# A fused cross-attention block in float32: its steps in a new order, and idle transposes in ten groups instead of two

## The chip, the cores and the metric

The kernel runs on one core of one Trainium2 chip. The metric is the device time of one execution in microseconds (us), as the median of several runs. Before the change it is 1016.84 us, the median of three runs between 1015.93 and 1018.15.

The core has five engines with instruction queues of their own: TensorE (PE in the profile; its weight loads stand apart as PEld), VectorE (DVE), ScalarE (ACT), GpSimd (POOL) and SyncE (SP), which here only issues DMAs. Each queue is worked off in the order of the program, and engines wait for one another by semaphores.

## The reference, cut to what matters

Queries come from `x` (16 batches of 1024 rows, 512 wide), keys and values from a context of 64 rows for each batch. Both are normalised and then scaled and shifted by a condition vector.

```python
def _ada_ln(x, c, W_ss, b_ss):
    mu = jnp.mean(x, axis=-1, keepdims=True)
    var = jnp.mean((x - mu) ** 2, axis=-1, keepdims=True)
    h = (x - mu) / jnp.sqrt(var + EPS)
    ss = jax.nn.silu(c) @ W_ss + b_ss
    scale, bias = jnp.split(ss, 2, axis=-1)
    return (1.0 + scale)[:, None, :] * h + bias[:, None, :]
...
xq = _ada_ln(x_q, t_vec, Wss_q, bss_q)
xkv = _ada_ln(x_kv, t_vec, Wss_kv, bss_kv)
q = (xq @ Wq + bq).reshape(B, Lq, nh, dh)
kv = (xkv @ Wkv + bkv).reshape(B, Lkv, 2, nh, dh)
...
scores = jnp.einsum('bqhd,bkhd->bhqk', q, k) / jnp.sqrt(jnp.float32(dh))
attn = jax.nn.softmax(scores, axis=-1)
out = jnp.einsum('bhqk,bkhd->bqhd', attn, v).reshape(B, Lq, H)
return x_q + (out @ Wp + bp)
```

There are 16 heads of width 32, and everything is float32.

## The kernel before

**Tiles.** The queries are cut into 32 blocks of 512 rows (`NB = 32`), two for each batch. The context is cut into two groups of eight batches, A and B, each as wide as one block. Features lie on the 128 partitions in four chunks (`NC = 4`).

**Seven products.** Each of the projections (keys, values, queries, output) is computed as seven half-size products in place of eight, from sums and differences of half matrices. `seven` (L551) does it for keys, values and queries, `product` (L911) for the output. Products 1, 6, 5 and 3 add up in one PSUM bank, 2 in one of its own, 7 and 4 in another, and what a bank holds is taken out between two products that add into it: `query_out` (ACT, L590) after 2, 6, 7 and 3, `query_added` (DVE, L597) after 5 and 4. So product 4 can start only when `query_out(n, 7)` has read the bank. Sums of features are made by `feature_sums` in four steps (L507; step 2 gives the operand of product 6, step 3 that of product 4), those of weights by `column_sums` (GpSimd, L481), those of attention rows by `row_sums` (GpSimd, L879 to L891).

**Way in.** `load_first` and `load_scale_shift` fetch the first context rows and the weights of scale and shift; `condition_turned` and `silu` prepare the condition; `q_stats`, `first_scale` and `hidden` normalise; `turned_features` transposes on TensorE; `scale_shift_rows`, `scale_shift_taken` and `scale_shift` make scale and shift; `modulated` applies them. Then come the 14 products of the context group A (`context_product`), mixed with those of query block 0, and those of group B, mixed with blocks 1 and 2. `biases(k)` transposes a few rows of biases into PSUM bank 1 on TensorE and copies them out on DVE (L236 to L243); the products k2 and k7 of group A use bank 1 too. `warm_up(n)` makes n transposes of the identity into a bank that nothing reads (L969).

**Loop.** `for i in range(3, NB - 2)` runs 27 times. In iteration i there are the scores of block i in two halves (`score_products`, L669), each with its column maxima (`maximum` on DVE, L686), a copy from PSUM to SBUF (`copied` on ACT, L695), an exchange of rows (`exchanged` on ACT, L724), `maxima` (DVE, L706 and L715), `subtract` (GpSimd, L732), `weights` (exponentials on ACT, L736) and `row_total` (DVE, L745); the mix with the values of block a = i - 1 (`mix`, L813), divided by its row sums (`inverse`, `spread_rows`, `divided` on DVE) and its output products 1, 2, 6, 5, 7; the output products 3 and 4 of block b = i - 2; the seven query products of block n = i + 1; and for later blocks the normalisation (`q_stats`, `q_scale`, `hidden`), a transposition by DVE and 16 DMAs (`turn`, `move`), scale and shift (`scale_features`, L456) and feature sums. `take` (ACT, L952) and `joined` (GpSimd, L957) bring an output product into the residual rows, as `added` (DVE, L931 and L936) does for others. The scores use both pairs of PSUM banks of the pool `ps_s`, and so does the mix: each waits until the copies and maxima, or `divided`, have emptied them.

**Way out.** Blocks y = 30 and z = 31 are written out by hand after the loop.

**What sets the order.** The order is written out: under `manual_schedule` each engine gets its instructions in the order in which the program's steps issue them. A step is a call such as `query_product(n, 4)`, and the change consists of such calls in another order.

Of the kernel before, what the change touches and what calls it, by code (L numbers as in the profile page):

```python
# [11 lines left out]
ALU = mybir.AluOpType  # L12
# [8 lines left out]
def cross_attention_block(  # L21
# [943 lines left out]
    warm = bank("warm", 1)  # L965

    def warm_up(n):
        for _ in range(n):
            nc.tensor.transpose(warm[:, :P], ident, ident)  # L969
# [39 lines left out]
    modulated("A", 1, 0, nc.vector)  # L1009
    turned_features("A", 2)  # L1010
    load_context_weights(1, 0, 1)
    modulated("A", 0, 1, nc.scalar)
    load_context_weights(0, 1)
    load_biases(1)
    load_scale_shift("q", w_ss_q, 0)
    load_scale_shift("q", w_ss_q, 1)
    q_stats(0, (3,))
    modulated("A", 1, 1, nc.vector)
    q_stats(0, (1,))
    q_stats(0, (2,))  # L1020
# [36 lines left out]
    hidden(0, (1,))
    hidden(0, (2,))
    context_out("A", "k", 6)
    q_stats("B", (2,))  # L1060
    q_stats("B", (1,))
    hidden(0, (0,))
    context_product("A", "k", 5)
    column_sums("q", w_q_sb, w_q_sums, (0,))
    turned_products()
    turned_scaled(0)
    context_out("A", "k", 5)
    context_out("A", "v", 1)
    load_x(1)
    context_product("A", "k", 3)  # L1070
    turned_scaled(1)
    q_stats("B", (3,))
    context_product("A", "v", 6)
    q_stats("B", (0,))
    context_out("A", "v", 2)
    turned_scaled(3)
    q_scale("B")
    context_out("A", "k", 4)
    context_out("A", "k", 3)
    context_product("A", "v", 7)  # L1080
    context_out("A", "v", 6)
    turned_scaled(2)
    hidden("B", (1,))
    hidden("B", (3,))
    query_product(0, 1)
    hidden("B", (0,))
    turned_features("B", 1)
    turned_features("B", 3)
    query_seed(0)
# [3 lines left out]
    turned_features("B", 0)  # L1093
    column_sums("q", w_q_sb, w_q_sums, (2,))
    hidden("B", (2,))
    query_product(0, 2)
    q_stats(1, (0,))
    q_stats(1, (2,))
    q_stats(1, (1,))
    q_stats(1, (3,))  # L1100
    q_scale(1)
    feature_sums(0, nc.gpsimd, (2,))
    column_sums("q", w_q_sb, w_q_sums, (1,))
    turned_features("B", 2)
    load_x(2)
    query_out(0, 2)
    modulated("B", 0, 0, nc.vector)
    modulated("B", 0, 1, nc.vector)
    context_out("A", "v", 7)
    hidden(1, (0,))  # L1110
    context_product("A", "v", 5)
    hidden(1, (3,))
    query_product(0, 7)
    context_product("A", "v", 4)
    modulated("B", 1, 1, nc.vector)
    hidden(1, (2,))
# [316 lines left out]
    for i in range(3, NB - 2):  # L1433
# [10 lines left out]
        if next_x:  # L1444
            q_stats(i + 4, (1,))
# [284 lines left out]
```

## Time and profile before

| what | value |
|---|---|
| median of three runs | 1016.84 us |
| the profiled execution | 1016.95 us |
| its span in the profile | 1015.1 us |
| busy: TensorE, DVE, GpSimd, ACT | 988.8, 920.1, 811.9, 771.1 us |
| way in, up to the first scores of block 3 | 160.3 us |
| loop, 27 iterations | 782.1 us |
| way out | 72.7 us |

The profiled execution took 1.85 us more than its span, which runs from the first instruction to the last. Times in the views are microseconds from the span's start. Busy time of TensorE is modelled: matmuls are pipelined and their shown lengths overlap, so a product's cost is read from start to start. A group's idle time is the wait of its engine just before it, with what ended that wait.

### The profile page before, as it was taken

To read this page: it belongs to the slowest core of one execution; us is meant where nothing else is said; L and a number is where in the kernel's file an instruction comes from. 1 tells how busy PE (TensorE), PEld (TensorE's weight loads), DVE (VectorE), ACT (ScalarE), POOL (GpSimd) and SP (SyncE) were. 2 spreads that over 40 slices of the span, in tenths; PEclk is the share of its full clock that TensorE was granted. 3 is DMA by queue.
4 is the path that set the end of the run, shared out by engine and by line. 5 is a ranking of instruction groups with operands and counts; after the bars stand their busy time and mean duration, and the time that the engine had idled before them with its cause. 6 is when DMAs were issued, how large, how long until landed. Compare 5 with 4: busy or idle time off the path is not lost. (4 is left out here: it accounts for less than half of the span.)

```text
span 1015.1 us, 17766 instructions
## 1 busy us (share of the span) xinstructions
PE 988.8 (97%) x6060; PEld 760.6 (75%) x6060; DVE 920.1 (91%) x1170; ACT 771.1 (76%) x1426; POOL 811.9 (80%) x603
## 2 busy tenths in 40 slices
PE   6999999999999999999999999999999999999998
PEld 5788777777777777777777777777777777777666
DVE  6589999999999999999999999999999999987895
ACT  3588775778888877788888777887887778886651
POOL 2476685988888889888888898888888988888794
PEclk9999999999999999999999999999999999999999
DMA  9465634455555445555545455555454455445223
GB/s 318 151 190 146 174 117 140 128 159 154 169 152 146 134 133 156 161 155 167 158 140 139 127 158 160 154 164 166 133 137 134 151 163 157 120 127 159 80 71 128
DMA packets 111802, 151.71 MB, mean 149 GB/s; under 512 B 29624, under 2 KB 45008, under 8 KB 111712
## 3 DMA queue, kind: packets, MB, share of 16 engines
q1 hardware_dynamic: 111024, 149.75, 49.6%
q8 instruction: 49, 0.80, 0.3%
q0 software_dynamic: 256, 0.52, 0.2%
q14 instruction: 41, 0.34, 0.1%
q10 hardware_dynamic: 432, 0.30, 0.1%
HBM read 80.26 MB, written 35.65 MB: 114 GB/s over the span
## 5 line engine op out<-in xcount | busy, mean ns | idle before, releaser
L732 POOL TENSOR_TENSOR s<-s,mb 128x2048 f32<-128x2048 f32 x64 | 290.9, 4545 | 31.7 <-DVE mb L715 29.2
L911 PE MATMUL pp<-w_p_sb,ot 128*128 128x256 f32 x760 | 178.9, 379 | 0.0
L957 POOL TENSOR_TENSOR r<-r,taken 128x512 f32<-128x512 f32 x116 | 146.8, 1277 | 23.5 <-ACT taken L952 23.3
L911 PEld LDWEIGHTS pp<-w_p_sb,ot 128*128 128x128 f32 x760 | 144.4, 190 | 19.7
L590 ACT ACTIVATE qt<-pq,bias_t 128x256 f32<-128x256 f32 x256 | 104.3, 474 | 70.6 <-PE pq L551 69.9
L686 DVE TRANSPOSE_TENSOR_REDUCE m<-ps 128x32 f32<-128x1024 f32 x128 | 155.5, 1219 | 2.1 <-ACT s L695 1.0
L715 DVE STREAM_TRANSPOSE mb<-m 128x2048 f32<-128x2048 f32 x64 | 147.9, 2312 | 7.0 <-POOL s L879 0.5
L745 DVE TRANSPOSE_TENSOR_REDUCE lt<-s 128x64 f32<-128x2048 f32 x64 | 143.8, 2278 | 5.1 <-ACT s L736 5.1
L695 ACT COPY s<-ps 128x1024 f32<-128x1024 f32 x128 | 126.9, 1015 | 23.6 <-POOL r L957 12.7
L736 ACT ACTIVATE s<-s 128x2048 f32<-128x2048 f32 x64 | 122.6, 1915 | 3.6 <-POOL s L732 3.5
L551 PE MATMUL pq<-xt,w_q_sb 128*128 128x256 f32 x512 | 124.1, 385 | 0.4 <-ACT pq L563 0.4
L911 PE MATMUL pp<-WT,ot 128*128 128x256 f32 x512 | 123.9, 385 | 0.0
L551 PEld LDWEIGHTS pq<-xt,w_q_sb 128*128 128x128 f32 x512 | 94.7, 190 | 36.5 <-issue 21.1
L911 PE MATMUL pp<-WT,s 128*128 128x256 f32 x512 | 121.2, 380 | 0.4 <-DVE r L936 0.4
L551 PE MATMUL pq<-xt,w_q_sums 128*128 128x256 f32 x512 | 121.2, 379 | 0.0
L911 PEld LDWEIGHTS pp<-WT,ot 128*128 128x128 f32 x512 | 94.9, 190 | 34.6 <-issue 21.9
L551 PE MATMUL pq<-xt_sums,w_q_sums 128*128 128x256 f32 x512 | 116.5, 379 | 0.5 <-ACT qt L590 0.5
L911 PEld LDWEIGHTS pp<-WT,s 128*128 128x128 f32 x512 | 97.0, 190 | 16.0 <-POOL r L957 1.3
L551 PEld LDWEIGHTS pq<-xt,w_q_sums 128*128 128x128 f32 x512 | 97.1, 190 | 14.8 <-ACT qt L590 0.8
L551 PEld LDWEIGHTS pq<-xt_sums,w_q_sums 128*128 128x128 f32 x512 | 97.2, 190 | 14.1 <-ACT qt L590 0.9
L347 ACT ACTIVATE x<-x,rstdq 128x512 f32<-128x512 f32 x128 | 103.9, 819 | 1.8 <-POOL rstdq L322 1.1
L952 ACT COPY taken<-pp 128x512 f32<-128x512 f32 x116 | 68.0, 586 | 47.3 <-PE pp L911 47.2
(172 smaller groups left out, 1611.4 us busy)
## 6 DMA issues: line engine op xcount, KB each, us to landing
x<-in_x_dram SPq DMA_DIRECT2D x32, 1024.0 KB, 5.1
r<-in_x_dram SPq DMA_DIRECT2D x32, 1024.0 KB, 6.8
out_dram<-r SPq DMA_DIRECT2D x62, 512.0 KB, 7.7
xt<-ht SPq DMA_DIRECT2D x488, 64.0 KB, 2.0
wss_kv<-in_L_xcond_Wss_kv_dram SPq DMA_DIRECT2D x4, 512.0 KB, 7.5
wss_q<-in_L_xcond_Wss_q_dram SPq DMA_DIRECT2D x4, 512.0 KB, 8.0
ltd<-lt SPq DMA_DIRECT2D x32, 64.0 KB, 1.5
vr<-ltd SPq DMA_DIRECT2D x126, 16.0 KB, 1.7
```

Of the source, the lines that this page charges most:

```text
L347: nc.scalar.activation(dst, src, AF.Identity, bias=rstd[:, 1, j : j + 1], scale=rstd[:, 0, j : j + 1])
L551: nc.tensor.matmul(out_, lhsT=lhsT, rhs=rhs, start=new and m == 0 and c == 0, stop=c == HC - 1, skip_group_check=True,)
L590: nc.scalar.activation(dst, src, AF.Identity, bias=bq_t[:, o : o + 1])
L686: nc.vector.tensor_reduce(m_tiles[i][:, z, 0, 2 * e : 2 * e + 2, :], s_banks[i, z][e].rearrange("p r (j a) -> p r j a", a=32), AX.X, ALU.m ...
L695: nc.scalar.copy(s_tiles[i, z][:, 2 * e : 2 * e + 2, :], s_banks[i, z][e])
L715: nc.vector.transpose(t, src.unsqueeze(2).to_broadcast([P, HPC * NJ, 32]))
L732: eng.tensor_tensor(s_tiles[i, w], s_tiles[i, w], mb_tiles[i, w], ALU.subtract)
L736: nc.scalar.activation(p, p, AF.Exp, scale=SCALE)
L745: nc.vector.tensor_reduce(lt_tiles[i][:, :, w, :], s_tiles[i, w].rearrange("p r (j a) -> p r j a", a=32), AX.X, ALU.add, apply_transpose=True,
L911: nc.tensor.matmul(acc[products_of(i, n)][:, t * HO : (t + 1) * HO], lhsT=rows[:, c, t * P : (t + 1) * P], rhs=cols[:, c, :], start=new an ...
L952: nc.scalar.copy(taken[i][:, slot, :], acc[products_of(i, n)])
L957: nc.gpsimd.tensor_add(r, r, taken[i][:, slot, :].rearrange("p (t h) -> p t h", t=2))
```

## The change

`warm_up` gets a bank as its second argument and takes a fresh tile on every call. It is called for 12, 4, 4, 3, 3, 4, 4, 4, 4 and 4 transposes between the first steps, where it was called for 12 and 6. All other steps of the way in, the loop and the way out are kept and stand in a new order; in the way in that covers loads too (the weights of scale and shift ahead of the key weights, the projection's weights earlier), and `context_product("A", "k", 1)` and `2` come before the first of the values. The diff, cut to the first steps, the loop and a part of the way out:

```diff
@@ -962,730 +962,740 @@
 
     w_k_sums = big.tile([P, 4, HC, HO], F32, tag="big2", name="w_k_sums")
     w_q_sums = qpool.tile([P, 4, HC, HO], F32, tag="wq", name="w_q_sums")
-    warm = bank("warm", 1)
-
-    def warm_up(n):
+    warmed = []
+
+    def warm_up(n, k=1):
+        warmed.append(n)
+        warm = bank(f"warm_{len(warmed)}", k)
         for _ in range(n):
             nc.tensor.transpose(warm[:, :P], ident, ident)
 
 
 
-    condition_turned()
-    load_first(2, 2)
+    warm_up(12)
     q_stats("A", (0,))
     q_stats("A", (1,))
-    warm_up(12)
-    warm_up(6)
+    warm_up(4, 2)
+    load_first(2, 2)
+    load_scale_shift("kv", w_ss_kv, 0, (1,))
     first_scale(0)
+    warm_up(4, 2)
+    warm_up(3)
+    condition_turned()
+    silu()
+    q_stats("A", (3,))
+    q_stats("A", (2,))
+    load_biases(0)
+    load_scale_shift("kv", w_ss_kv, 1, (0,))
+    warm_up(3)
+    warm_up(4, 2)
+    biases(0)
+    warm_up(4, 2)
     load_scale_shift("kv", w_ss_kv, 0, (0,))
-    load_context_weights(0, 0, 0)
-    q_stats("A", (2,))
-    hidden("A", (1,))
-    q_stats("A", (3,))
-    silu()
+    load_scale_shift("kv", w_ss_kv, 1, (1,))
     first_scale(1)
     hidden("A", (0,))
-    turned_features("A", 0)
+    load_biases(1)
+    warm_up(4, 2)
     hidden("A", (2,))
-    load_scale_shift("kv", w_ss_kv, 0, (1,))
+    warm_up(4, 2)
+    warm_up(4, 2)
+    hidden("A", (1,))
+    turned_features("A", 1)
     scale_shift_rows("kv", 0)
     hidden("A", (3,))
     scale_shift_taken("kv", 0)
+    scale_shift("kv", 2 * NC, 0)
+    modulated("A", 0, 0, nc.scalar)
+    load_context_weights(0, 0, 0)
+    scale_shift_rows("kv", 1)
     load_context_weights(0, 0, 1)
-    turned_features("A", 3)
-    load_context_weights(1, 0, 0)
-    load_scale_shift("kv", w_ss_kv, 1, (0,))
-    load_biases(0)
-    biases(0)
-    load_scale_shift("kv", w_ss_kv, 1, (1,))
-    turned_features("A", 1)
-    scale_shift("kv", 2 * NC, 0)
-    scale_shift_rows("kv", 1)
-    load_x(0)
-    modulated("A", 0, 0, nc.vector)
+    turned_features("A", 0)
+    turned_features("A", 2)
+    modulated("A", 0, 1, nc.vector)
     scale_shift_taken("kv", 1)
     scale_shift("kv", 2 * NC, 1)
-    modulated("A", 0, 0, nc.scalar)
+    modulated("A", 0, 0, nc.vector)
+    modulated("A", 1, 0, nc.scalar)
+    biases(1)
+    turned_features("A", 3)
+    load_context_weights(0, 1)
+    load_context_weights(1, 0, 0)
+    context_product("A", "k", 1)
     modulated("A", 1, 0, nc.vector)
-    turned_features("A", 2)
+    modulated("A", 1, 1, nc.scalar)
+    column_sums("k", w_k_sb, w_k_sums, (0,))
+    modulated("A", 0, 1, nc.scalar)
+    context_product("A", "k", 2)
+    load_x(0)
+    context_product("A", "v", 1)
+    modulated("A", 1, 1, nc.vector)
+    column_sums("k", w_k_sb, w_k_sums, (1,))
+    column_sums("k", w_k_sb, w_k_sums, (2,))
+    feature_sums("A", nc.vector, (0,))
+    feature_sums("A", nc.vector, (1,))
+    load_scale_shift("q", w_ss_q, 0)
+    feature_sums("A", nc.vector, (2,))
+    context_out("A", "k", 1)
+    context_out("A", "k", 2)
+    q_stats(0, (0,))
+    feature_sums("A", nc.vector, (3,))
+    q_stats(0, (3,))
+    context_product("A", "k", 6)
+    context_product("A", "k", 7)
...
     for i in range(3, NB - 2):
         a, b, n, f = i - 1, i - 2, i + 1, i + 2
         more, next_x = i < NB - 3, i + 4 < NB
 
         score_products(i, 0)
-        product(b, 3)
+        if next_x:
+            q_stats(i + 4, (1,))
+        copied(i, 0, 1)
+        query_product(n, 1)
+        query_seed(n)
         maximum(i, 0, 0)
-        query_product(n, 1)
-        copied(i, 0, 1)
-        added(b, 3)
+        copied(i, 0, 0)
         maximum(i, 0, 1)
         if next_x:
-            q_stats(i + 4, (1,))
-        product(b, 4)
-        copied(i, 0, 0)
+            q_stats(i + 4, (3,))
+        product(b, 3)
+        added(b, 3)
+        query_product(n, 2)
+        score_products(i, 1)
         exchanged(i, 0)
-        score_products(i, 1)
-        query_seed(n)
         maxima(i, 0)
         maximum(i, 1, 0)
+        subtract(i, 0)
         inverse(a)
+        query_out(n, 2)
+        query_product(n, 6)
         if more:
             hidden(i + 3, (1,))
+        product(b, 4)
+        if more:
+            hidden(i + 3, (2,))
+        query_out(n, 6)
         maximum(i, 1, 1)
-        subtract(i, 0)
-        query_product(n, 2)
-        query_product(n, 6)
-        query_out(n, 2)
         query_product(n, 7)
+        spread_rows(a)
         copied(i, 1, 0)
+        copied(i, 1, 1)
+        query_out(n, 7)
+        added(b, 4)
+        mix(a)
+        divided(a, (0,))
+        query_product(n, 4)
+        exchanged(i, 1)
+        biased(a, 2)
+        divided(a, (1,))
+        weights(i, 0)
+        maxima(i, 1)
+        row_sums(a, 0, (0,))
         if more:
             hidden(i + 3, (3,))
-        spread_rows(a)
-        added(b, 4)
-        copied(i, 1, 1)
-        mix(a)
-        divided(a, (0,))
-        row_sums(a, 0, (0,))
-        divided(a, (1,))
-        exchanged(i, 1)
-        query_out(n, 7)
-        query_out(n, 6)
-        maxima(i, 1)
-        biased(a, 2)
-        weights(i, 0)
+        if more:
+            turn(i + 3, (3,))
+        product(a, 1)
+        query_added(n, 4)
         row_sums(a, 1, (0,))
         if more:
+            turn(i + 3, (2,))
+        if more:
+            turn(i + 3, (1,))
+        if more:
             hidden(i + 3, (0,))
-        query_product(n, 4)
-        product(a, 1)
+        if more:
+            turn(i + 3, (0,))
+        if i < NB - 5:
+            load_x(i + 5)
         product_seed(a)
         query_product(n, 5)
-        if more:
-            hidden(i + 3, (2,))
+        query_added(n, 5)
+        row_sums(a, 0, (1,))
+        subtract(i, 1)
         scale_features(f, (0,))
+        product(a, 6)
+        scale_features(f, (3,))
+        product(a, 2)
+        scale_features(f, (2,))
+        take(a, 6, 2)
+        take(a, 2, 0)
+        row_total(i, 0)
+        biased(a, 3)
+        product(a, 5)
+        weights(i, 1)
         if next_x:
             q_stats(i + 4, (0,))
-        if more:
-            turn(i + 3, (2,))
-        product(a, 2)
-        scale_features(f, (2,))
-        take(a, 2, 0)
+        if next_x:
+            q_stats(i + 4, (2,))
+        take(a, 5, 3)
+        joined(a, 6, 2)
+        query_product(n, 3)
         if i == NB - 3:
             load_residual(NB - 1)
-        if more:
-            turn(i + 3, (0,))
-        product(a, 6)
-        row_sums(a, 0, (1,))
-        query_added(n, 5)
-        biased(a, 3)
-        take(a, 6, 2)
-        query_product(n, 3)
-        if more:
-            turn(i + 3, (3,))
-        product(a, 5)
-        subtract(i, 1)
+        joined(a, 2, 0)
+        query_out(n, 3)
+        product(a, 7)
+        row_total(i, 1)
+        sums_moved(i)
         scale_features(f, (1,))
-        joined(a, 2, 0)
-        joined(a, 6, 2)
-        row_sums(a, 1, (1,))
-        if next_x:
-            q_stats(i + 4, (2,))
-        if more:
-            turn(i + 3, (1,))
-        product(a, 7)
-        weights(i, 1)
-        take(a, 5, 3)
-        if next_x:
-            q_stats(i + 4, (3,))
-        query_out(n, 3)
-        if i < NB - 5:
-            load_x(i + 5)
         joined(a, 5, 3)
-        scale_features(f, (3,))
-        row_total(i, 0)
         take(a, 7, 1)
         joined(a, 7, 1)
+        feature_sums(f, nc.gpsimd, (0,))
+        feature_sums(f, nc.gpsimd, (1,))
+        row_sums(a, 1, (1,))
+        feature_sums(f, nc.gpsimd, (2,))
+        if i + 3 < NB:
+            move(i + 3)
         if next_x:
             q_scale(i + 4)
-        row_total(i, 1)
-        feature_sums(f, nc.gpsimd, (0,))
-        feature_sums(f, nc.gpsimd, (1,))
-        query_added(n, 4)
-        feature_sums(f, nc.gpsimd, (2,))
+        load_residual(i)
         feature_sums(f, nc.gpsimd, (3,))
-        sums_moved(i)
-        if i + 3 < NB:
-            move(i + 3)
-        load_residual(i)
 
...
-    maximum(z, 0, 0)
+    row_sums(y - 1, 0, (1,))
+    product(y - 1, 1)
+    row_sums(y - 1, 1, (0,))
     copied(z, 0, 1)
     maximum(z, 0, 1)
+    query_added(z, 4)
+    product(y - 1, 2)
     weights(y, 1)
-    query_added(z, 4)
-    product(y - 1, 1)
-    row_sums(y - 1, 0, (1,))
+    subtract(y, 0)
     copied(z, 0, 0)
+    row_total(y, 1)
+    exchanged(z, 0)
+    biased(y, 2)
+    maxima(z, 0)
+    weights(y, 0)
+    row_total(y, 0)
+    row_sums(y - 1, 1, (1,))
     take(y - 1, 1, 0)
-    exchanged(z, 0)
-    product(y - 1, 2)
-    subtract(y, 0)
-    weights(y, 0)
+    score_products(z, 1)
+    sums_moved(y)
+    subtract(z, 0)
+    product(y - 2, 4)
+    product(y - 1, 6)
     take(y - 1, 2, 1)
-    row_total(y, 1)
-    maxima(z, 0)
-    score_products(z, 1)
-    row_sums(y - 1, 1, (0,))
+    take(y - 1, 6, 3)
+    maximum(z, 1, 1)
     joined(y - 1, 1, 0)
-    row_total(y, 0)
-    product(y - 1, 6)
-    sums_moved(y)
-    maximum(z, 1, 1)
     maximum(z, 1, 0)
-    product(y - 2, 4)
-    added(y - 2, 4)
-    take(y - 1, 6, 3)
-    subtract(z, 0)
-    load_residual(y)
     biased(y - 1, 3)
     copied(z, 1, 1)
+    product(y - 1, 5)
+    product(y - 1, 7)
+    added(y - 2, 4)
     exchanged(z, 1)
-    product(y - 1, 7)
-    row_sums(y - 1, 1, (1,))
+    joined(y - 1, 2, 1)
+    weights(z, 0)
+    copied(z, 1, 0)
+    take(y - 1, 5, 1)
+    mix(y)
+    take(y - 1, 7, 2)
     maxima(z, 1)
-    joined(y - 1, 2, 1)
-    copied(z, 1, 0)
-    weights(z, 0)
+    subtract(z, 1)
+    row_total(z, 0)
+    product(y - 1, 4)
     inverse(y)
     spread_rows(y, (0,))
-    take(y - 1, 7, 2)
+    weights(z, 1)
+    product(y - 1, 3)
+    divided(y, (0,))
     spread_rows(y, (1,))
-    mix(y)
-    biased(y, 2)
-    product(y - 1, 5)
-    product(y - 1, 4)
-    divided(y, (0,))
-    take(y - 1, 5, 1)
...
```

More of the change, by code (lines that the diff above doesn't have):

```diff
@@ L1060, in cross_attention_block @@
-    q_stats("B", (2,))
-    q_stats("B", (1,))
[L1062 to L1069, printed above, removed]
-    context_product("A", "k", 3)
[L1071 to L1076, printed above, removed]
+    column_sums("k", w_k_sb, w_k_sums, (3,))
@@ L1100, in cross_attention_block @@
[L1100 to L1105, printed above, removed]
-    query_out(0, 2)
[L1107 to L1116, printed above, removed]
+    context_out("A", "v", 7)
@@ L1283, in cross_attention_block @@
[L1283 to L1300 removed]
+    query_product(2, 1)
+    feature_sums(2, nc.gpsimd, (0,))
+    context_out("B", "v", 1)
@@ new lines, in cross_attention_block @@
+    q_scale(4)
+    row_total(0, 0)
+    query_seed(2)
+    context_product("B", "v", 2)
+    exchanged(1, 1)
+    hidden(4, (2,))
+    context_out("B", "v", 2)
+    copied(1, 1, 1)
+    copied(1, 1, 0)
+    move(3)
+    context_product("B", "v", 6)
+    query_product(2, 2)
+    maxima(1, 1)
+    scale_features(3, (2,))
+    context_product("B", "v", 7)
+    q_stats(5, (2,))
+    feature_sums(2, nc.gpsimd, (1,))
+    q_stats(5, (1,))
+    scale_features(3, (0,))
+    query_out(2, 2)
+    feature_sums(2, nc.gpsimd, (2,))
@@ L1314, in cross_attention_block @@
-    turn(4, (1,))
-    row_sums(0, 0)
-    query_out(2, 7)
-    biased(0, 2)
+    mix(0)
     query_added(2, 5)
     query_product(2, 3)
+    feature_sums(3, nc.gpsimd, (0,))
+    divided(0)
+    value_move("B", 1)
+    weights(1, 0)
+    row_total(1, 0)
+    feature_sums(3, nc.gpsimd, (1,))
+    query_product(2, 4)
+    query_out(2, 3)
+    row_sums(0, 0)
+    feature_sums(3, nc.gpsimd, (2,))
+    query_added(2, 4)
+    score_products(2, 0)
+    maximum(2, 0, 1)
+    product(0, 2)
+    weight_sums(0)
@@ L1320, in cross_attention_block @@
+    query_product(3, 1)
+    weight_sums(1)
+    turn(4, (0,))
+    weights(1, 1)
+    copied(2, 0, 0)
+    maximum(2, 0, 0)
+    copied(2, 0, 1)
+    nc.gpsimd.tensor_tensor(b_diff, b_second, b_first, ALU.subtract)
+    row_sums(0, 1)
+    exchanged(2, 0)
+    turn(4, (3,))
     product(0, 1)
-    load_residual(0)
-    maxima(1, 0)
+    weight_sums(3)
+    score_products(2, 1)
     row_total(1, 1)
-    load_x(6)
-    row_sums(0, 1)
-    query_out(2, 3)
-    weight_sums(0)
-    score_products(2, 0)
@@ L1341, in cross_attention_block @@
-    query_added(2, 4)
-    exchanged(2, 0)
-    added(0, 6)
-    query_product(3, 1)
-    q_stats(6, (0,))
-    query_seed(3)
-    maxima(2, 0)
-    weights(1, 0)
-    biased(0, 3)
-    hidden(5, (0,))
+    q_scale(5)
+    query_out(3, 2)
+    biased(0, 3)
+    query_out(3, 6)
+    exchanged(2, 1)
+    q_stats(6, (1,))
+    query_product(3, 7)
+    hidden(5, (0,))
+    copied(2, 1, 1)
+    sums_moved(1)
+    added(0, 6)
+    product(0, 7)
+    inverse(1)
     move(4)
-    feature_sums(3, nc.gpsimd, (0,))
@@ L1353, in cross_attention_block @@
[L1353 removed]
+    added(0, 7)
+    spread_rows(1)
     product(0, 5)
[L1355 to L1369 removed]
+    copied(2, 1, 0)
+    subtract(2, 0)
+    hidden(5, (3,))
+    query_out(3, 7)
@@ L1370, in cross_attention_block @@
+    added(0, 5)
+    product(0, 4)
+    query_product(3, 5)
+    product(0, 3)
+    weights(2, 0)
+    maxima(2, 1)
+    q_stats(6, (2,))
+    query_added(3, 5)
+    mix(1)
+    subtract(2, 1)
+    added(0, 3)
+    added(0, 4)
+    divided(1)
+    hidden(5, (1,))
+    biased(1, 2)
     hidden(5, (2,))
-    subtract(2, 0)
-    copied(2, 1, 0)
+    query_product(3, 3)
+    weights(2, 1)
+    product(1, 1)
+    q_stats(6, (3,))
     turn(5, (0,))
-    query_product(3, 7)
-    added(0, 5)
-    query_product(3, 6)
```

589 lines of the change are left out of this document (264 added, 325 removed).

## Prediction

> **What bounds the kernel now.** I read the page first, then who waited for whom, then TensorE's timeline in three places: the way in, one period of the loop, the way out.
>
> ```profile
> span 1015.1 us, 17766 instructions
> ...
> PE 988.8 (97%) x6060; PEld 760.6 (75%) x6060; DVE 920.1 (91%) x1170; ACT 771.1 (76%) x1426; POOL 811.9 (80%) x603
> ```
>
> TensorE is busy for 97% of the span, so the change, which adds and removes no product, can win only what TensorE loses: waits, and time at a lower clock. The waits of TensorE, in the view of who waited for whom (us in total, times, longest), begin so:
>
> ```profile
> PE pq L551 <- ACT qt L590: 5.6, 27, 0.9
> ...
> PE pk_A L551 <- DVE bias_t L241: 2.0, 1, 2.0
> ```
>
> The first is one wait in each iteration of the loop, the last is one stall in the way in. Here is TensorE's timeline in the way in (start, us, operation, in brackets the idle time before it), and then two windows behind the stall (stretch and its length, TensorE's busy time and instructions, granted clock, DMA share, GB/s):
>
> ```profile
> 5.65 3.51 PE L969 MATMUL warm<-ident 128*128 128x128 f32 x18
> 11.68 1.02 PE L411 MATMUL pxk_A<-ident,x_A 128*128 128x128 f32 x4 [2.52 <-DVE x_A L357]
> ...
> 20.08 0.65 PE L411 MATMUL pxk_A<-ident,x_A 128*128 128x128 f32 x4 [1.52 <-DVE xk_A L428]
> 20.57 1.89 PE L551 MATMUL pk_A<-xk_A,w_k_sb 128*128 128x256 f32 x8
> ...
> 28.04 2.92 PE L551 MATMUL pk_A<-xk_A,w_k_sb 128*128 128x256 f32 x8 [1.96 <-DVE bias_t L241]
> 30.75 4.39 PE L551 MATMUL pk_A<-xk_sums_A,w_k_sums 128*128 128x256 f32 x16
> 35.07 1.96 PE L266 MATMUL ss_q<-wss_q,early 128*32 128x128 f32 x64
> ...
> 64.95 1.89 PE L551 MATMUL pq<-xt,w_q_sums 128*128 128x256 f32 x8
> 66.68 1.89 PE L551 MATMUL pk_B<-xk_B,w_k_sb 128*128 128x256 f32 x8
> ```
> ```profile
> 28.00:30.00 2.00, 1.96 (x7) 0.72 1.07 363
> 30.00:32.00 2.00, 2.00 (x6) 0.50 1.06 385
> ```
>
> A product at full clock takes 66.68 - 64.95 = 1.73 us from start to start. After the stall of 1.96 us the granted clock falls to 0.50, and the next three products take 35.07 - 28.04 = 7.03 us instead of 5.19. The stall therefore costs 1.96 + 1.84 = **3.8 us**. From 28.04 to 66.68 there is no other gap of note.
>
> Now the loop: one period, the loop's ends, and a place in the way out where the operation after `mix` doesn't wait.
>
> ```profile
> 160.30 1.11 PE L669 MATMUL ps<-qt,K_A 32*64 32x512 f32 x16
> ...
> 711.04 1.11 PE L669 MATMUL ps<-qt,K_B 32*64 32x512 f32 x16
> ...
> 718.51 1.99 PE L551 MATMUL pq<-xt,w_q_sb 128*128 128x256 f32 x8
> ...
> 723.89 1.95 PE L813 MATMUL po<-s,V_B 64*32 64x512 f32 x32
> 725.99 1.97 PE L551 MATMUL pq<-xt_sums,w_q_sb 128*128 128x256 f32 x8 [0.16 <-ACT qt L590]
> ...
> 739.97 1.11 PE L669 MATMUL ps<-qt,K_B 32*64 32x512 f32 x16
> ...
> 942.37 1.11 PE L669 MATMUL ps<-qt,K_B 32*64 32x512 f32 x16
> ...
> 956.41 1.95 PE L813 MATMUL po<-s,V_B 64*32 64x512 f32 x32
> 958.29 1.99 PE L551 MATMUL pq<-xt,w_q_sums 128*128 128x256 f32 x8
> ```
>
> 27 iterations take 942.37 - 160.30 = 782.07 us, 28.97 each. The period shown is 28.93. From `mix` to the next product it takes 2.10 us, and without a wait 1.88 (956.41 to 958.29): 0.22 of the period is the wait, and **28.71** is TensorE's floor.
>
> **The change part by part.** *Way in.* Before, the second bias transpose shares bank 1 with product k2, and its DVE copies stand behind three feature sums, so k2 waits. Now `biases(1)` stands ahead of `context_product("A", "k", 1)`, its copies ahead of the sums, and k2 finds its bank free. That removes the 3.8 us above, if the first product starts when it did. Will it? Its path (statistics, normalise, scale and shift, modulate) keeps its operations; the condition is turned later, the scale and shift loads now precede all of w_k, and `hidden("A", (1,))` stands behind the second `first_scale`. The start could gain the 1.5 us that TensorE waited at 20.08, or lose about as much as the old stall, 1.9. I take 0, the middle. The loads behind it (x_0, w_q, x_B) keep their sizes; w_q comes last in both orders. Also new is that k6 follows v1 and needs the third feature sum. I take no wait there (bounds 0 and 1 us).
>
> The 46 transposes of the identity run where TensorE waits for loads or for normalised rows, until 11.68 in the old trace. The 18 of before took 3.51 / 18 = 195 ns each; 46 at that price are 9.0 us, and they no longer wait for the condition's load. I cost them at nothing; should they end late, the last two groups, 8 transposes, would be 1.6 us on the path.
>
> *From 66.68 to 160.30* the same operations stand in another order, TensorE has one wait of half a microsecond, and I take 0, between -0.6 and +3.
>
> *Loop.* Before, `query_out(n, 7)`, for which q4 waits, since it adds into the same bank, stands on ScalarE behind two score copies, a `hidden` and the four copies of `exchanged`. Now it stands directly behind the score copies, `exchanged` after it, and a second query product's output goes ahead of them. By the rows, with 0 at the start of the first scores: q7 ends where `mix` starts, at 723.89 - 711.04 = 12.85; `query_out(n, 7)` takes half of the 1.57 us below and ends at 13.7; q4 is due 1.88 after `mix`, at 14.7. The wait goes. What is late next? The closest is q6. It moves up from third to first behind the second scores, due at 718.51 - 711.04 = 7.47, and needs the third feature sum. On GpSimd `row_sums(a, 1, (1,))` now stands ahead of that sum, and `q_scale` behind it. The rows of ScalarE and GpSimd that price this:
>
> ```profile
> 711.33 0.59 ACT L952 COPY taken<-pp 128x512 f32<-128x512 f32 x1
> ...
> 725.01 1.57 ACT L590 ACTIVATE qt<-pq,bias_t 128x256 f32<-128x256 f32 x4
> ```
> ```profile
> 712.07 1.26 POOL L957 TENSOR_TENSOR r<-r,taken 128x512 f32<-128x512 f32 x1 [0.71 <-ACT taken L952]
> ...
> 714.29 1.27 POOL L507 TENSOR_TENSOR xt_sums<-xt 128x512 f32<-128x512 f32 x1
> ...
> 716.99 1.27 POOL L507 TENSOR_TENSOR xt_sums<-xt 128x512 f32<-128x512 f32 x1
> ```
>
> (The 1.35 us from start to start come from the last two: two sums in 2.70.) The last product of the period ends at about 0.07; `take` 0.59 and 0.1 to GpSimd; then `joined`, two feature sums, the row sum and the third feature sum: five operations at 1.27 to 1.35 from start to start, 6.4 to 6.7. It ends between 7.2 and 7.5: q6 doesn't wait, by a hair. I take the floor, 27 x 28.71 = 775.2, a gain of **6.9 us**; no gain beyond that is to be had.
>
> *Way out* (0 at 942.37). Its waits before:
>
> ```profile
> 967.63 1.11 PE L669 MATMUL ps<-qt,K_B 32*64 32x512 f32 x16
> ...
> 974.84 1.09 PE L813 MATMUL po<-s,V_B 64*32 64x512 f32 x16 [0.72 <-ACT s L695]
> 977.00 1.09 PE L813 MATMUL po<-s,V_B 64*32 64x512 f32 x16 [1.07 <-ACT s L695]
> ...
> 989.18 1.97 PE L911 MATMUL pp<-WT,s 128*128 128x256 f32 x8 [0.38 <-DVE r L936]
> ```
> ```profile
> L732 POOL TENSOR_TENSOR s<-s,mb 128x2048 f32<-128x2048 f32 x64 | 290.9, 4545 | 31.7 <-DVE mb L715 29.2
> ...
> L686 DVE TRANSPOSE_TENSOR_REDUCE m<-ps 128x32 f32<-128x1024 f32 x128 | 155.5, 1219 | 2.1 <-ACT s L695 1.0
> ...
> L745 DVE TRANSPOSE_TENSOR_REDUCE lt<-s 128x64 f32<-128x2048 f32 x64 | 143.8, 2278 | 5.1 <-ACT s L736 5.1
> L695 ACT COPY s<-ps 128x1024 f32<-128x1024 f32 x128 | 126.9, 1015 | 23.6 <-POOL r L957 12.7
> L736 ACT ACTIVATE s<-s 128x2048 f32<-128x2048 f32 x64 | 122.6, 1915 | 3.6 <-POOL s L732 3.5
> ```
>
> Up to `score_products(z, 1)` at 25.3 the order gives the same waits. Behind it stand four products instead of three ahead of `mix(y)`, and the mix needs `copied(z, 1, 0)`, which now stands at the end of a chain (mean durations of the groups): `subtract(y, 0)` starts behind three row sums at about 21.0 and takes 4.5; `weights(y, 0)` 1.9; `row_total(y, 0)`, behind `maxima(z, 0)` on DVE until 28.1, 2.3; two maxima 2.4; `exchanged` 1.0; `weights(z, 0)` 1.9; the copy 1.0: 36.7. TensorE is there at 25.3 + 1.15 + 4 x 1.73 + 0.75 (product 5 waits for a `take`) = 34.1, say 34.3. That makes waits of 0.75 + 2.4 = 3.15 us, against 0.72 + 1.07 + 0.38 and some 0.3 of restarts before. **+0.6 us** (an estimate; bounds -1.5 and +2).
>
> *Sum*, against the profiled execution's own 1016.95 us: 1016.95 - 3.8 - 6.9 + 0.6 = **1006.9 us**. The median of the three runs, 1016.84, is 0.1 lower and leaves that as it is.
>
> **The rivals.** *The wait only moves to q6.* The hair above is 0 to 0.3 us. If GpSimd starts its chain 0.3 us later than I worked out, because ScalarE's `take` stands behind a late `query_out(n, 3)`, the period goes back to 28.97 and the 6.9 are lost: 1013.8. Against it: `take` was ready in time in the old order too, with one scale ahead of it.
>
> *The clock falls in the way in all the same.* TensorE still waits twice for modulated rows before the first product, and in the trace 1.96 us was enough; if the clock falls as the products start, that is the 1.84 us again: 1008.7. For it: two waits together are as long as the old one. Against it: a wait of 1.52 us (ahead of 20.08) left the clock alone. The Trainium skill (TensorE: Matmul & The Clock Gate, "HAM oscillation — how this bites in real kernels") puts the harmful gap above some 3.4 us; by that rule this rival falls away and its chance goes to the forecast. The trace, where 1.96 us were enough, disagrees, so the rival stays.
>
> *The way in gains nothing.* The first product starts 1.9 us later and 1.9 are lost between the first products, where k6 now waits for sums: 1010.7.
>
> *Slower: the loop hangs on DVE.*
>
> ```profile
> 711.04:739.97 28.93, 28.77 (x177) 21.99 (x176) 27.18 (x34) 23.56 (x44) 24.86 (x19) 1.00 0.51 150
> ```
>
> DVE (the third busy time of the row, behind TensorE and its weight loads) works 27.18 of 28.93 us. There is a ring: `maxima(i, 1)` on DVE, `subtract(i, 1)` on GpSimd (4.5), `weights(i, 1)` on ScalarE (1.9), `row_total(i, 1)` on DVE, and round again. The new order puts four turns, two additions, a row total and two statistics on DVE beside the leg on the other engines, so the ring closes in 27.2 us plus a short wait for product 3. It decides when DVE idles over 28.71 - 27.18 = 1.5 us in each iteration; at 2.0 us the period is 29.17, 5.4 us over the loop's present 27 iterations, and the kernel ends at 1016.95 - 3.8 + 0.6 + 5.4 = 1019.1. Against it: DVE would have to wait in several places at once.
>
> **How the numbers follow.** Forecast 0.50, clock 0.15, way in without gain 0.11, wait at q6 0.17, DVE's ring 0.07. About 0.2% (2 us) is what a measurement of this kernel can tell from no change. Faster by more than that are the first three and most of the fourth, 0.88; the rest of the fourth, where some of the way in is lost too, is within 0.2%, 0.05; slower 0.07. The range goes from 1003.5 (the first product 1.5 earlier, the way out 1.5 better) to 1013.8, the case of the wait at q6, and leaves out its worse half and the ring.
>
> **What would show it.** Right: no wait of `pk_A` for `bias_t`, a granted clock of 1.00 from the first product on, `pk_B` first at about 63; scores 28.71 apart in the loop, no wait of `pq` for `qt`; a wait of about 2 us ahead of the second last mix. Wrong: a wait of `pq` for `xt_sums` on GpSimd in each iteration, half a clock after 20 us, or a loop in which DVE has no idle time.

## The result and the profile after

The changed kernel takes **1008.8 us** (median, 1008.47 to 1009.57), against 1016.38 us (1015.59 to 1018.15) for the kernel before on the same chip. The ratio is 0.9924, with an interval of 0.9907 to 0.9941. The forecast was 1006.9, so the sign and most of the size were right, and about 2 us of the gain are missing.

The profiled execution took 1008.77 us. Its page, and the longest waits of TensorE in the view of who waited for whom (us in total, times, longest):

```profile
span 1007.0 us, 17791 instructions
...
PE 991.7 (98%) x6088; PEld 763.0 (76%) x6088; DVE 918.7 (91%) x1170; ACT 773.3 (77%) x1426; POOL 809.6 (80%) x603
```
```profile
PE ps_kv L288 <- DVE early L279: 1.8, 2, 1.4
PE pxk_A L411 <- ACT xk_A L430: 1.6, 1, 1.6
...
PE pq L551 <- ACT qt L590: 0.7, 1, 0.7
```

Both of the old waits have left the list as they stood there: `pk_A` no longer waits for `bias_t`, and `pq` waits for `qt` once, in the way out, instead of 27 times (26 of them in the loop, one in the way out). The longest waits are now in the way in, among the operations ahead of the first product. What the two spans spent in each stretch, cut by the starts of the same operations on TensorE:

| stretch | before | after | gain | forecast |
|---|---|---|---|---|
| way in, to the first product of `pk_B` | 66.68 | 64.80 | 1.88 | 3.8 |
| from there to the first scores of the loop | 93.62 | 93.20 | 0.42 | 0 |
| loop, 27 iterations | 782.07 | 775.75 | 6.32 | 6.9 |
| way out, to the end of the span | 72.73 | 73.25 | -0.52 | -0.6 |
| span | 1015.1 | 1007.0 | 8.10 | 10.1 |

So the loop and the way out came out nearly as forecast, and the way in gave half of what it should. TensorE's timeline there (start, us, operation, in brackets the idle time before it), and the windows around the first product (stretch and length, TensorE's busy time and instructions, granted clock, DMA share, GB/s):

```profile
8.45 2.80 PE L971 MATMUL warm<-ident 128*128 128x128 f32 x16
11.96 0.66 PE L411 MATMUL pxk_A<-ident,x_A 128*128 128x128 f32 x4 [0.72 <-ACT x_A L347]
...
18.25 0.33 PE L288 MATMUL ps_kv<-ident,early 128*128 128x128 f32 x1 [1.39 <-DVE early L279]
...
20.28 1.12 PE L411 MATMUL pxk_A<-ident,x_A 128*128 128x128 f32 x4 [1.55 <-ACT xk_A L430]
21.19 4.67 PE L551 MATMUL pk_A<-xk_A,w_k_sb 128*128 128x256 f32 x16
25.70 1.89 PE L551 MATMUL pv_A<-w_v_sb,xk_A 128*128 128x256 f32 x8
...
64.80 1.89 PE L551 MATMUL pk_B<-xk_B,w_k_sb 128*128 128x256 f32 x8
```
```profile
20.00:22.00 2.00, 1.72 (x6) 0.50 1.09 352
22.00:24.00 2.00, 2.00 (x8) 0.67 1.09 348
24.00:26.00 2.00, 2.00 (x11) 1.00 1.09 363
```

The stall of 1.96 us is gone, and no operation of TensorE from `k1` (21.19) to the loop waits. But TensorE stands idle twice ahead of it, for 1.39 and 1.55 us, and the granted clock falls to 0.50 just as the products begin. From the last four transposes to `k1` it takes 21.19 - 20.28 = 0.91 us instead of 20.57 - 20.08 = 0.49, and `k1` and `k2` together take 25.70 - 21.19 = 4.51 us instead of 2 x 1.73 = 3.46. The half clock thus costs 0.42 + 1.05 = 1.47 us. Of the 1.84 us behind the old stall most has thus not been won back: the half clock now stands at the first products.

In the loop, the period that answers to the one shown of before, on TensorE, GpSimd and ScalarE, and its window (TensorE, weight loads, VectorE, ScalarE, GpSimd, then clock, DMA share, GB/s):

```profile
703.90 1.11 PE L669 MATMUL ps<-qt,K_B 32*64 32x512 f32 x16
...
711.36 1.99 PE L551 MATMUL pq<-xt_sums,w_q_sums 128*128 128x256 f32 x8
...
716.74 1.95 PE L813 MATMUL po<-s,V_B 64*32 64x512 f32 x32
718.62 1.99 PE L551 MATMUL pq<-xt_sums,w_q_sb 128*128 128x256 f32 x8
...
732.63 1.11 PE L669 MATMUL ps<-qt,K_B 32*64 32x512 f32 x16
```
```profile
709.82 1.28 POOL L507 TENSOR_TENSOR xt_sums<-xt 128x512 f32<-128x512 f32 x1
```
```profile
716.85 0.84 ACT L590 ACTIVATE qt<-pq,bias_t 128x256 f32<-128x256 f32 x2 [0.43 <-PE pq L551]
717.71 1.00 ACT L724 COPY m<-m 32x64 f32<-32x64 f32 x4
```
```profile
703.90:732.63 28.73, 28.73 (x178) 21.98 (x177) 27.31 (x34) 23.64 (x43) 24.80 (x18) 1.00 0.52 152
```

The period is 732.63 - 703.90 = 28.73 us, and TensorE is busy for all of it. ScalarE runs `query_out(n, 7)` at 716.85 and only then the four copies of `exchanged` (L724), so `qt` is taken at 717.69, 0.93 us before q4 starts, and from `mix` to q4 it is 1.88 us with no wait. On GpSimd the third feature sum ends at 709.82 + 1.28 = 711.10, which is 0.26 us ahead of q6 at 711.36: the "hair" of the forecast.

### The profile page after: what moved, and what is told of

Same layout as the page of the kernel before. It is cut to its first block, busy times and chain, and to the rows that moved or that the text cites. A ratio compares the mean times of both kernels' runs of the same rounds, so it can differ in the third digit from the quotient of the medians.

```text
span 1007.0 us, 17791 instructions
## 1 busy us (share of the span) xinstructions
PE 991.7 (98%) x6088; PEld 763.0 (76%) x6088; DVE 918.7 (91%) x1170; ACT 773.3 (77%) x1426; POOL 809.6 (80%) x603
## 4 chain that ended last, share of the span: by engine, by line
PE 93%; DVE 3%; ACT 1%; issue 1%; DMA 1%; POOL 1%; DVEq 0%; ACTq 0%; POOLq 0%
PE pq L551 38%; PE pp L911 37%; PE ps L669 6%; PE po L813 6%; PE pk_A L551 1%; PE pv_B L551 1%; PE pk_B L551 1%; PE pv_A L551 1%; DVE mb L715 0%; DVE lt L745 0%; DVE m L686 0%; DMA x_A<-in_ctx_dram 0%; POOL xt L398 0%; DVE ot L799 0%; DVE ht L378 0%
## 5 line engine op out<-in xcount | busy, mean ns | idle before, releaser
L590 ACT ACTIVATE qt<-pq,bias_t 128x256 f32<-128x256 f32 x256 | 107.1, 472 | 82.1 <-PE ps L669 55.8
L745 DVE TRANSPOSE_TENSOR_REDUCE lt<-s 128x64 f32<-128x2048 f32 x64 | 147.1, 2298 | 10.4 <-ACT s L736 10.4
L551 PE MATMUL pq<-xt_sums,w_q_sums 128*128 128x256 f32 x512 | 123.9, 385 | 0.7 <-ACT qt L590 0.7
L551 PEld LDWEIGHTS pq<-xt_sums,w_q_sums 128*128 128x128 f32 x512 | 94.8, 190 | 35.7 <-POOL workq L319 20.3
L911 PE MATMUL pp<-WT,ot 128*128 128x256 f32 x512 | 121.1, 379 | 0.0
L911 PEld LDWEIGHTS pp<-WT,ot 128*128 128x128 f32 x512 | 97.1, 190 | 14.1 <-issue 0.8
L347 ACT ACTIVATE x<-x,rstdq 128x512 f32<-128x512 f32 x128 | 96.8, 804 | 2.2 <-POOL rstdq L322 2.1
```

The lines of the kernel that those rows point to most:

```text
L347: nc.scalar.activation(dst, src, AF.Identity, bias=rstd[:, 1, j : j + 1], scale=rstd[:, 0, j : j + 1])
L551: nc.tensor.matmul(out_, lhsT=lhsT, rhs=rhs, start=new and m == 0 and c == 0, stop=c == HC - 1, skip_group_check=True,)
L590: nc.scalar.activation(dst, src, AF.Identity, bias=bq_t[:, o : o + 1])
L745: nc.vector.tensor_reduce(lt_tiles[i][:, :, w, :], s_tiles[i, w].rearrange("p r (j a) -> p r j a", a=32), AX.X, ALU.add, apply_transpose=True,
L911: nc.tensor.matmul(acc[products_of(i, n)][:, t * HO : (t + 1) * HO], lhsT=rows[:, c, t * P : (t + 1) * P], rhs=cols[:, c, :], start=new an ...
```

## The experiments

My theory after the traces: the loop's gain comes wholly from the place of `exchanged(i, 1)` behind `query_out(n, 7)`; the way in's gain comes from the bias copies that now stand ahead of the feature sums, less a half clock that the two idle gaps bring back. Rivals: the loop needed the rest of its new order too; the half clock comes from something else, such as the late bias load; the 46 transposes themselves set the time. The runs came in two groups, each on a chip of its own, with runs of the kernel before on the same chip (medians 1017.12 us for the first four kernels and 1017.78 for the other four). Ratios are to these.

### One line in the way in

The kernel before, with only the second bias transposes moved up.

```diff
     modulated("A", 1, 1, nc.scalar)
+    biases(1)
     feature_sums("A", nc.vector, (0,))
...
     feature_sums("A", nc.vector, (2,))
-    biases(1)
     context_out("A", "k", 1)
```

> The old order with one step moved: biases(1) ahead of the first feature sum. Theory: the stall of product k2 is the wait for the bias copies on DVE, and it alone brought the half clock behind it. Then the wait of pk_A for bias_t is gone, the granted clock is 1.00 from 26 to 34 us, pk_B starts at about 62.9 instead of 66.68, and the time is 3.8 us less, 1012.6. Rival, a gap of 2 us doesn't cool the array and the half clock has another cause: 2.0 us less, 1014.4, with the half clock still there. Rival, the stall is replaced by the next late thing (the third feature sum, which is now 0.5 us later): under 1 us less.

Measured: 1014.32 us, ratio 0.9974 (0.9961 to 0.9987). TensorE in its way in:

```profile
19.93 0.66 PE L411 MATMUL pxk_A<-ident,x_A 128*128 128x128 f32 x4 [1.52 <-DVE xk_A L428]
...
25.96 1.89 PE L551 MATMUL pk_A<-xk_A,w_k_sb 128*128 128x256 f32 x8
...
63.45 1.89 PE L551 MATMUL pk_B<-xk_B,w_k_sb 128*128 128x256 f32 x8
...
101.23 1.99 PE L551 MATMUL pv_B<-wv_sums,xk_sums_B 128*128 128x256 f32 x8 [1.13 <-DVE stage_B L631]
```

`k2` starts at 25.96 without a wait, no product from `k1` on runs at half rate, and `pk_B` starts 66.68 - 63.45 = 3.23 us earlier. In this execution the half clock went together with the old stall. A part of the gain is lost again behind `pk_B`: the wait for `stage_B` is 1.13 us instead of 0.59, another of 0.25 (for `K_B`) is new, and the first scores of the loop come at 158.13 instead of 160.30, so only 2.17 us earlier. By the medians the gain is 2.8 us, with an interval of 1.3 to 4.0. That is less than the 3.8 expected; the interval holds the rival's 2.0 as well, and it is the trace, without half rate behind `k2`, that speaks against the rival.

### One line in the loop

The kernel before, with only this:

```diff
         divided(a, (1,))
-        exchanged(i, 1)
         query_out(n, 7)
+        exchanged(i, 1)
```

> The old order with one step moved in the loop: exchanged(i, 1) behind query_out(n, 7). Theory: this one place held the product q4 in each iteration. Scores then start 28.72 apart instead of 28.97, pq doesn't wait for qt in the loop, and the time is 6.3 to 6.9 us less, about 1009.8. Rival, the whole new order of the loop is needed, since maxima(i, 1) and what follows now come 0.85 us later: period 28.9, time 1016.

Measured: 1011.32 us, ratio 0.9944 (0.9927 to 0.9961). Its wait for `qt`, its way in, and one window of it:

```profile
PE pq L551 <- ACT qt L590: 0.5, 1, 0.5
```
```profile
22.04 1.12 PE L411 MATMUL pxk_A<-ident,x_A 128*128 128x128 f32 x4 [1.52 <-DVE xk_A L428]
22.94 3.62 PE L551 MATMUL pk_A<-xk_A,w_k_sb 128*128 128x256 f32 x8
26.36 4.42 PE L551 MATMUL pv_A<-w_v_sb,xk_A 128*128 128x256 f32 x16
```
```profile
22.00:24.00 2.00, 1.96 (x7) 1.00 1.06 339
```

The wait is gone from all iterations (the one left is in the way out). The loop ran from 162.41 to 938.58, so 776.17 us or 28.75 each, against 28.73 in the changed kernel and 28.97 before. One swapped pair of lines gives 782.07 - 776.17 = 5.90 of the loop's 6.32 us. The rest of the loop's new order is worth at most 0.4 us.

### Both lines

> The old order with both single moves. If the two causes are independent: 1016.4 - 3.8 - 6.5 = 1006.1, which would be under the changed kernel's 1008.8. If the earlier way in only runs into another wait in front of the loop: as the loop's move alone, 1009.8.

Measured: 1008.57 us, ratio 0.992 (0.9898 to 0.9941), level with the changed kernel's 0.9924. In the profile the loop takes 776.16 us and `pk_B` starts at 64.30. By the medians the two lines gain 2.8 and 5.8 us alone and 1017.12 - 1008.57 = 8.55 together, so they add up; the 1006.1 expected counted the first at 3.8. Two lines give as much as the whole new order and the 28 more transposes gave. This run also showed something that I had not looked for:

```profile
19.97 1.12 PE L411 MATMUL pxk_A<-ident,x_A 128*128 128x128 f32 x4 [1.52 <-DVE xk_A L428]
20.88 2.88 PE L551 MATMUL pk_A<-xk_A,w_k_sb 128*128 128x256 f32 x8
```

The same gap of 1.52 us, at the same place as in the kernel with the first line alone, is here followed by half rate: the four transposes take 1.12 us instead of 0.66, and `k1` 2.88 instead of 1.89.

### Idle work in the two gaps

The changed kernel, with 23 more idle transposes where TensorE waits ahead of the first product.

```diff
     turned_features("A", 2)
+    warm_up(11, 2)
     modulated("A", 0, 1, nc.vector)
...
     biases(1)
+    warm_up(12, 2)
     turned_features("A", 3)
```

> The new order with 23 more transposes of the identity in TensorE's two gaps ahead of the first product (11 behind turned_features A2, 12 behind biases(1)). Theory: gaps of 1.39 and 1.55 us brought the half clock under k1 and k2, which cost 1.06 us. Then the clock stays 1.00 from 18 to 24 us, k1 starts at 21.2 as before, v1 at 24.7 instead of 25.7, and the time is 1.0 less, 1007.8. Rival, gaps under 3.4 us don't cool the array: the half clock stays and the time is 1008.8. If the transposes end late they delay scale_shift and k1: 1009 to 1010.

Measured: 1005.99 us, ratio 0.9896 (0.9878 to 0.9914). Four of the five runs lie between 1005.86 and 1007.53; the fifth, 1008.8, is the profiled one. The median is 1.8 us below the 1007.8 expected; the changed kernel was not run on this chip, so the comparison goes by the ratios, 0.9896 against 0.9924. In the profiled execution the first bias load landed late, and the transposes behind it ran at half rate:

```profile
9.25 0.24 PE L236 MATMUL pb<-ident,early 8*128 8x8 f32 x1 [1.59 <-DMA early<-in_L_xcond_bss_kv_dram]
9.42 4.63 PE L971 MATMUL warm<-ident 128*128 128x128 f32 x16
13.85 1.06 PE L411 MATMUL pxk_A<-ident,x_A 128*128 128x128 f32 x4
...
23.63 3.62 PE L551 MATMUL pk_A<-xk_A,w_k_sb 128*128 128x256 f32 x16
```

The 16 transposes took 4.63 instead of 2.80 us and held up the first context transposes by about 1.9 us (13.85 against 11.96). `k1` and `k2`, behind the filled gaps, ran at full rate (3.62 us) even so, so the late load is not what halves the rate under them. This is the case in which the idle transposes lie on the path.

### The changed kernel again, and with the old way out

In the second group the changed kernel ran again, unaltered, beside the filled one in which the steps behind the loop stand in the order of before.

> The changed kernel once more, beside its variants and the kernel before on one chip: 0.992 of the time before, 1008.8, if chip and run make no difference. If the way in depends on how the clock's windows fall, single runs spread by 1 to 2 us, and so does the place where the rows show half rate.

> The changed kernel with the 23 added transposes and with the old order of the way out. Theory: the old way out is 0.5 us shorter (72.7 against 73.25), nothing else changes: 0.5 less than the kernel with the 23 transposes, 1005.5. Rival, the way out's length depends on the loop's end, and the old order is no better behind the new loop: 1006.0.

Measured: 1009.43 us for the changed kernel (1005.97 to 1011.56), ratio 0.9916 (0.9896 to 0.9936); 1006.12 us for the other, ratio 0.9892 (0.9875 to 0.991), with four of five runs between 1006.05 and 1006.33 and one at 1008.31. First the changed kernel, then the filled one, with one of its windows:

```profile
21.23 5.84 PE L551 MATMUL pk_A<-xk_A,w_k_sb 128*128 128x256 f32 x16
26.90 1.89 PE L551 MATMUL pv_A<-w_v_sb,xk_A 128*128 128x256 f32 x8
```
```profile
16.59 1.36 PE L971 MATMUL warm<-ident 128*128 128x128 f32 x11
...
18.57 1.53 PE L971 MATMUL warm<-ident 128*128 128x128 f32 x12
20.18 0.66 PE L411 MATMUL pxk_A<-ident,x_A 128*128 128x128 f32 x4
20.67 3.62 PE L551 MATMUL pk_A<-xk_A,w_k_sb 128*128 128x256 f32 x16
24.13 1.89 PE L551 MATMUL pv_A<-w_v_sb,xk_A 128*128 128x256 f32 x8
...
63.20 1.89 PE L551 MATMUL pk_B<-xk_B,w_k_sb 128*128 128x256 f32 x8
```
```profile
20.00:22.00 2.00, 1.91 (x12) 1.00 1.10 352
```

In this execution of the changed kernel `k1` and `k2` lose 26.90 - 21.23 - 3.46 = 2.2 us, in the first one they lost 1.05: the same code with the same two gaps. (The kernel of the last experiment below has this way in too, and loses 25.53 - 21.08 - 3.46 = 0.99.) The mean granted clock of the six executions goes the same way: the two at 1.000 took 1005.97 and 1007.3 us, the four at 0.995 to 0.998 between 1009.05 and 1011.56, though the clock record is not complete (see the last section).

With the gaps filled they lose nothing, and `pk_B` starts at 63.20, where the forecast had put it ("about 63"), 1.60 us before the changed kernel's 64.80. The half clock in front of and under `k1` and `k2`, 1.47 us, is thus the larger part of what the way in missed.

The filled kernel is also the steadier one: the changed kernel's best run, 1005.97, is as good, but its other five are 1.3 to 5.6 us slower. The two intervals overlap (0.9896 to 0.991), so the 3.3 us between the medians are likely rather than certain; both measurements of the changed kernel gave 0.992, both filled versions 0.989 to 0.990.

At full rate the loop starts at 156.43 in this profile and at 158.13 in the one with the bias line alone, so between these two profiles the rest of the new order, with its gaps filled, is worth 1.7 us ahead of the loop. No run filled the gap of the kernel with two lines. The two filled versions are the fastest kernels that I found.

As for the way out: from the first scores behind the loop to the end of the span this kernel takes 1004.5 - 932.18 = 72.32 us, the changed one 73.25 and 73.05 in its two profiles. That does not show the old way out to be shorter, since the first filled kernel, with the new one, takes 1006.9 - 935.13 = 71.8 us. The difference lies in the last store. It took 3.3 us from issue to landing in the changed kernel's first profile, and in the first filled kernel's (DMA issues at the end: how many, KB each, median us to landing):

```profile
out_dram<-r SPq DMA_DIRECT2D x2, 128.0 KB, 1.8
```

Up to the start of the last product the new order takes 66.19 us in all its profiles and the old one 65.78 here, so by that measure the old way out is 0.4 us shorter. The medians of the two filled kernels, on different chips, can't tell that apart.

### Fewer transposes

The changed kernel with 18 idle transposes (12 and 6) instead of 46, everything else in its new place.

```diff
     warm_up(12)
     q_stats("A", (0,))
     q_stats("A", (1,))
-    warm_up(4, 2)
+    warm_up(6)
...
-    warm_up(4, 2)
-    warm_up(3)
     condition_turned()
...
```

> The changed kernel with 12 and 6 idle transposes at the head (18 in two groups) instead of 46 in ten. Theory: the added 28 keep TensorE busy until the normalised rows come; without them it idles from about 6 to 12 us, the scale and shift rows run at half rate, k1 starts up to 1 us later and k1 and k2 are at half rate for longer: 1 to 2 us more than the changed kernel, 1010.3. Rival, the transposes do nothing, since the array falls to half rate at 19 us with them too: same time, 1008.8.

Measured: 1010.62 us (1008.79 to 1011.97), ratio 0.9929 (0.9911 to 0.9948), beside the changed kernel's 1009.43 (0.9896 to 0.9936) in the same group. The difference of 1.2 us is not settled by these intervals. The profile:

```profile
11.76 1.12 PE L411 MATMUL pxk_A<-ident,x_A 128*128 128x128 f32 x4 [3.33 <-ACT x_A L347]
12.80 1.94 PE L266 MATMUL ps_kv<-wss_kv,early 128*32 128x128 f32 x32
...
23.89 5.17 PE L551 MATMUL pk_A<-xk_A,w_k_sb 128*128 128x256 f32 x16
```

Without the later groups TensorE waits 3.33 us for the first normalised rows and then computes the scale and shift at half rate, 1.94 us for 32 products against 1.08. `k1` starts at 23.89 instead of 21.23. In this profile the clock was thus not up between 12 and 18 us; with all the transposes it was in both profiles of the changed kernel, though not in the first filled one, where the transposes themselves ran at half rate. Whether that is worth 1 or 2 us in the median stays open.

### The margin at q6

The changed kernel, with the four small operations of `q_scale` ahead of the third feature sum on GpSimd, as a trial of the rival "the wait only moves to q6".

```diff
         row_sums(a, 1, (1,))
+        if next_x:
+            q_scale(i + 4)
         feature_sums(f, nc.gpsimd, (2,))
         if i + 3 < NB:
             move(i + 3)
-        if next_x:
-            q_scale(i + 4)
```

> The changed kernel with q_scale(i + 4) one place earlier on GpSimd in the loop, ahead of the third feature sum. The sum ends 0.26 us before q6 is due in the changed kernel; q_scale's four operations take 1.0 us. Theory: q6 waits, the period is 28.73 + 0.74 = 29.47, 26 iterations give 19 us, the time is 1028: the new order stands within 0.3 us of a bound on GpSimd. Rival, the wait is taken up elsewhere in the ring (GpSimd idles 3.9 us in each period): under 5 us more.

Measured: 1026.83 us, ratio 1.0091 (1.0064 to 1.0119). The waits of TensorE and GpSimd's timeline:

```profile
PE pq L551 <- POOL xt_sums L507: 17.4, 25, 0.7
```
```profile
723.39 0.20 POOL L319 TENSOR_TENSOR workq<-workq 128x4 f32<-128x4 f32 x1
...
724.38 1.27 POOL L507 TENSOR_TENSOR xt_sums<-xt 128x512 f32<-128x512 f32 x1
```

The four operations take 724.38 - 723.39 = 0.99 us, the margin was 0.26, and q6 waits 0.70 in each of 25 iterations. The loop takes 794.86 instead of 775.75 us: 19.1 us lost. The rival was a real one; the changed kernel stays clear of it by a quarter of a microsecond.

## Why the forecast was nearly right, step by step

**The old stall: nearly right.** Of its price of 1.96 + 1.84 most was found again: the bias line alone moved `pk_B` by 3.23 us, and with the gaps filled it moved by 66.68 - 63.20 = 3.48.

**Way in, -3.8: the term that was mis-sized.** It measured 1.88. The step that failed is "if the first product starts when it did", together with the chance of 0.15 for the rival "the clock falls in the way in all the same". That rival came true, and with it the sign that the forecast had named for it, half a clock after 20 us. Its time, 1008.7, is what was measured, but the parts differ: it counted 1.84 for the clock. Of the 1.92 us missing, 1.47 are half clock (0.42 on the last transposes, 1.05 on `k1` and `k2`), and 0.20 are the transposes' later start (20.28 instead of 20.08). The rest, 0.25, I did not trace to one place. The evidence that I set against the rival was that "a wait of 1.52 us (ahead of 20.08) left the clock alone". One execution was too little for that: the same 1.52 us halved the rate in the kernel with both lines and left it alone in the kernel with the first.

The Trainium skill (TensorE: Matmul & The Clock Gate, "HAM oscillation — how this bites in real kernels") warns of idle gaps above some 3.4 us. Here no gap ahead of the products was over 1.55 us, and two of them, 2.94 us within 20.28 - 16.86 = 3.42, were enough; the trace disagrees with that reading. The same page ("Part 1: The HAM clock gate") says that the clock is judged over a free-running window, so that the point of a change varies from run to run, by about half a microsecond either way. Here the spread is wider. The granted clock reads 0.67 from 22 to 24 us in the changed kernel's first profile and 0.57 from 24 to 26 in its second, so the half clock ended near 23.3 in the one and near 25.7 in the other. The rule fits a gap that sometimes costs 0 and sometimes a half clock, and one kernel losing 1.05 and 2.2 us in two profiles; no run here shows the window itself.

**Middle, 0: off by 0.42.** The one wait that stood there before is not among the waits of the changed kernel:

```profile
103.40 1.99 PE L551 MATMUL pv_B<-wv_sums,xk_sums_B 128*128 128x256 f32 x8 [0.59 <-DVE stage_B L631]
```

**Transposes at nothing: right where I looked, with a caveat.** They end at 8.45 + 2.80 = 11.25 and TensorE then waits 0.72 for `x_A`. With a late bias load at half rate they were on the path, for 1.9 us against the 1.6 that I named as the bound.

**Loop, -6.9: right.** It measured 6.32; the period is 28.73 where I had 28.71. The third feature sum was worked out to end 7.2 to 7.5 us into the period and ended at 711.10 - 703.90 = 7.20; q6 was due at 7.47 and came at 7.46. The ring over VectorE didn't decide: TensorE is busy for the whole period and waits for nothing. That VectorE idles for 28.73 - 27.31 = 1.42 us shows nothing by itself, as it is only what its work leaves of the period.

**Way out, +0.6: right sum, by luck.** It measured +0.52, but the same order measured 71.8 us in the first filled kernel, which is 0.9 less than before. Without the last store, up to the start of the last product, it costs 66.19 against 65.89, so +0.30. I had put waits of 0.75 (product 5, for a `take`) and 2.4 (ahead of the mix) behind the last scores, which stand at 958.81. The timeline shows:

```profile
964.25 1.99 PE L911 MATMUL pp<-WT,s 128*128 128x256 f32 x8 [0.68 <-ACT taken L952]
...
967.90 1.09 PE L813 MATMUL po<-s,V_B 64*32 64x512 f32 x16
969.84 1.09 PE L813 MATMUL po<-s,V_B 64*32 64x512 f32 x16 [0.85 <-ACT s L695]
...
975.30 1.99 PE L911 MATMUL pp<-w_p_sb,ot 128*128 128x256 f32 x8 [0.70 <-DVE ot L799]
```

The wait of product 5 came as forecast, 0.68. TensorE reached the mix as forecast too, at 967.90 - 933.75 = 34.2, but its first half runs without a wait, and only the second half waits for the copy. TensorE reached that half at 969.84 - 0.85 - 933.75 = 35.2, and the copy came at about 36.1 rather than 36.7, so the wait was 0.85 instead of 2.4. The 0.70 of the product that needs `ot` was not in my sum at all. Errors in opposite directions made the total look exact.

**The range.** Its lower end is not the sum of what it names: 1.5 us for the first product and 2.1 for the way out (from +0.6 to -1.5) lead from 1006.9 to 1003.3, not 1003.5. Nothing hangs on it.

## What to carry to other kernels

When a large reordering gains, look for the one or two waits that it removes and try them alone: here two moved lines gave as much as a rewritten order, which went further only with its gaps filled. Price a stall of TensorE with the half clock that may follow it, and expect a gap of 1.5 us ahead of the first products to cost that in some executions; idle products in the gap are a cheap cover. Work out the margin of the operation that becomes critical next, since 0.26 us of it stood between a gain of 6 us and a loss of 13 in the loop.

## What the hardware showed that I had not expected

**The clock row can read 1.00 while products run at half rate.** With the loop line alone, `k1` took 26.36 - 22.94 = 3.42 us from start to start instead of 1.73, and the window over it shows a granted clock of 1.00. The four transposes ahead of it took 1.12 us instead of 0.66, so the half rate began earlier, and the record shows no change of the clock in that stretch. The kernel with few transposes shows it too: 32 products took 1.94 us instead of 1.08 at 12.80, and the window from 12 to 14 us reads 1.00. Durations of equal instructions are the safer reading there.

**The way in isn't the same twice.** The wait for the first bias load was 0.44 us in the changed kernel's first profile, and 1.90 in its second. There it cost nothing by itself, as the next transposes ran at full rate. In the two profiles `pk_B` starts at 64.80 and 66.00, while the loops agree to 0.01 us (775.75 in both). At the other end the last store took 1.8 us in some profiles and 3.3 in another.
